# Dividing the softmax in the rows of `wo`: values and sums moved by DMA, reciprocal and product there, in place of two rounds of transposes

## The chip, the cores and the metric

The kernel runs on one core of a Trainium2 chip. The core has a matrix engine (TensorE, PE in the profile), three engines for elementwise work (VectorE or DVE, ScalarE or ACT, GpSimd or POOL), an engine that here only issues transfers (SyncE or SP) and 16 DMA engines. The metric is the time of one execution on the device in microseconds; lower is better. Everything is computed in float32.

## The reference

The input `x` has 8 sequences of 512 tokens with 256 features. Four residual blocks follow each other: attention with 16 heads of 16 features, a feed-forward block, a linear attention with a decay mask over groups of 512 tokens, and the same feed-forward block again. Only the first block bears on the change:

```python
q = x @ Wq + bq
kv = (x @ Wkv_down + bkv_down) @ Wkv_up + bkv_up
# split into k and v, 16 heads of 16 features; rotary embedding on q and k
att = jnp.einsum('bhqd,bhkd->bhqk', q, k) / jnp.sqrt(HEAD_DIM)
att = att + (log_sparse + jnp.log(decay + 1e-09))
att = jax.nn.softmax(att, axis=-1)          # the division of this softmax is what is changed
out = jnp.einsum('bhqk,bhkd->bhqd', att, v)
out = out + 0.2 * sigmoid(q . mean(k)) * mean(v)
return out.reshape(B, T, 256) @ Wo + bo
```

The division of the softmax is done after the product with `v`: a column of ones beside the values makes the same matmul give the sum of the unnormalised probabilities, and values are then divided by sums.

## The kernel before, in words

**Work items.** A batch (sequence) `b` has four groups `g` of four heads; item `i = 4 b + g` is one group, 32 items in all. A group has four blocks `t` of 128 tokens and two pairs of heads, so an item has 8 steps and the kernel has 256. In a step PE computes one pair's scores twice: `s` with queries in the rows, of which DVE takes the row maximum (`reduce_item`, tile `mr`), and, ten steps later for the same block and pair, `t` with keys in the rows, of which ACT takes the exponential into tile `p` (`soft_item`); DVE, or POOL in one step of three, then multiplies `p` by the table `dec_a`, two instructions of 128x512. Every second step `pv_item` adds a block's four heads into `pv`, one PSUM bank of 128 rows: 32 rows for each head, of which the first 16 are values and row 16 is the sum. `vaug` (tile `va`) is the stationary side of that matmul; in before a head has 17 columns in it, 16 values and a one. There is one `pv` bank.

**After an item.** `post_units(i)` makes the work that follows an item's last `pv` matmul. `evacuate` copies `pv` into `num` on ACT. `divide` turns `num` with four PE transposes (`flip`, line 201) into a PSUM tile with tokens in the rows, where the 16 sums of a token lie beside its values; a DVE reciprocal of 128x16 and a DVE product of 128x256 write `atok`. After every second item `turn` turns a half of `atok` back with four more transposes, and ACT copies the result into `aT`, features in the rows, as the product with `wo` wants it. `wo_unit` (two for each batch) then multiplies `aT` with `wo_sb`, adds the memory term (tiles `ga`, `me`), and DVE adds the residual.

**Order.** The order of instructions on each engine is fixed when the program is built: every instruction is pinned in program order. A planner at the end of the kernel decides it. It keeps a clock for each engine, and interleaves the 256 steps with chains of `Unit`s: the front of the next batches, the rest of earlier ones (feed-forward, linear attention), and `posts`, the units from `post_units`, which come first. A `Unit` names its estimated PE time, then the engines and nanoseconds that follow (`then`); units without PE time are issued as soon as the planner's PE clock comes within 300 ns of their start. `step_start` holds a step back until the planner's clocks say its PSUM banks and its `p` tiles are ready.

A unit may also have `needs`, names that another unit `gives`. A name is given at the moment at which the giving unit is issued, not at its estimated end:

```python
if any(x not in given for x in u.needs) or any(a.done is None for a in u.after):
    return None
...
t = max([a.done for a in u.after] + [clock["PE"] if u.pe else 0])
```

`wo_unit` stands in such a relation: `wos[0].needs = (("aT", b),)`, and the last unit of item `4 b + 3` gives `("aT", b)`.

**Transfers.** `move` (line 91) issues a DMA from SP's queue, in program order. It carries the loads, the way of rotated queries and keys through DRAM (`dq`, `dk`) and back into `qT` and `kT`, the loads of the next `x`, and the results. In PSUM, `s` and `t` share two tiles of two banks (`ps_sc`), one bank is `pv`, three are `misc`.

Of the kernel before, what the change touches and what calls it, by code (L numbers as in the profile page):

```python
# [9 lines left out]
F32 = mybir.dt.float32  # L10
AF = mybir.ActivationFunctionType
ALU = mybir.AluOpType
# [3 lines left out]
P = 128  # L16
B, T, D = 8, 512, 256
NH, HD = 16, 16
HH = 8
NG = 4  # L20
NT = T // P
NC = D // P
# [13 lines left out]
def tile_kernel(  # L36
# [37 lines left out]
    dve, act, gps = Engine(nc.vector), Engine(nc.scalar), Engine(nc.gpsimd)  # L74
# [4 lines left out]
    at = ctx.enter_context(tc.tile_pool(name="at", bufs=2))  # L79
    rs = ctx.enter_context(tc.tile_pool(name="rs", bufs=2))  # L80
# [9 lines left out]
    def move(to, src):  # L90
        tc.keep_in_program_order(nc.sync.dma_start(to, src))
# [11 lines left out]
    def keep(shape, name):  # L103
        return const.tile(shape, F32, tag=name, name=name)
# [24 lines left out]
    bv, b2 = row[:, 0, :], row[:, 1, :]  # L129
# [2 lines left out]
    qT = [keep([P, NG, T], f"qT{i}") for i in range(2)]  # L132
    kT = [keep([P, NG, T], f"kT{i}") for i in range(2)]

    vaug = [keep([P, NT, NH * 17 + 15], f"va{i}") for i in range(2)]

    mrow = [keep([P, NG, NT], f"mr{i}") for i in range(2)]

# [58 lines left out]
    def mm(o, l, r, start=True, stop=True):  # L197
        tc.keep_in_program_order(nc.tensor.matmul(o, lhsT=l, rhs=r, start=start, stop=stop))  # L198

    def flip(o, i):  # L200
        tc.keep_in_program_order(nc.tensor.transpose(o, i, ident))  # L201

    def misc(name):
        return ps_m.tile([P, 512], F32, tag="m", name=name)
# [39 lines left out]
    bb = const.tile([P, 5], F32, tag="bb", name="bb")  # L244
    wr = {}

    def plain(j):
        ps = misc(f"wr{j}")
        for o in range(NC):
            for c in range(NC):  # L250
                flip(ps[:, o * D + c * P : o * D + (c + 1) * P], wqk_in[:, c, j, o * P : (o + 1) * P])
        wr[j] = rs.tile([P, NC, D], F32, tag="xr", bufs=3, name=f"wr{j}")
        act.copy(wr[j].rearrange("p o d -> p (o d)"), ps)

    def product():
# [81 lines left out]
    def front1(b):  # L337
        def latent():
            ps = misc(f"lat_{b}")
            for c in range(NC):  # L340
                mm(ps[:LAT, :], wd_sb[:, c, :], xT_a[b]["xT"][:, c, :], c == 0, c == NC - 1)
            lt = fr.tile([LAT, T], F32, tag="lat", name=f"lat_{b}")
            lsum[b] = fr.tile([LAT, 1], F32, tag="lsum", name=f"lsum_{b}")
            act.activation(lt, ps[:LAT, :], AF.Identity, bias=vec[:LAT, V_BD : V_BD + 1], accum_out=lsum[b])
            lat_a[b] = lt

        def values(h):
            ps = misc(f"v_{b}_{h}")
            for i in range(2):
                t = 2 * h + i  # L350
                mm(ps[:, i * D : (i + 1) * D], lat_a[b][:, t * P : (t + 1) * P], wv_sb)
            for i in range(2):
                dve.tensor_tensor(
                    vaug[b % 2][:, 2 * h + i, : NH * 17].rearrange("p (h d) -> p h d", d=17)[:, :, :HD],
                    ps[:, i * D : (i + 1) * D].rearrange("p (h d) -> p h d", d=HD),
                    bv.rearrange("p (h d) -> p h d", d=HD),
                    ALU.add,
                )


        def mean_v():
            ps = misc(f"mv_{b}")
            for c in range(NC):
                mm(ps[:, c : c + 1], wv_sb[:, c * P : (c + 1) * P], lsum[b])
            m = fr.tile([P, NC], F32, tag="mv_a", name=f"mv_a_{b}")
            dve.scalar_tensor_tensor(m, ps[:, :NC], 0.1 / T, bvc, ALU.mult, ALU.add)
            for c in range(NC):
                gps.tensor_scalar(vmean[:, c, : NH + 1], vmask[:, c, :], m[:, c : c + 1], None, ALU.mult)

        def through_wo():  # L370
            ps = misc(f"me_{b}")
            for c in range(NC):
                mm(ps[:, :D], vmean[:, c, :], wo_sb[:, c, :], c == 0, c == NC - 1)
            dve.tensor_add(mem[b % 2][: NH + 1, :], ps[: NH + 1, :D], bo_row[: NH + 1, :])

        s, (h0, h1) = ln_units(lambda: xs[b], f"a{b}", fr)
        free = PER * (b - 1) + LAG + PVLAG + 2
        u = {"lat": Unit(latent, 1720, (("ACT", 700),), after=[h0[2], h1[2]])}
        for h in range(2):
            u["v", h] = Unit(  # L380
                lambda h=h: values(h), 900, (("DVE", 850),), after=[u["lat"]], step=free
            )
        u["mv"] = Unit(mean_v, 250, (("DVE", 150), ("POOL", 400)), after=[u["lat"]])
        u["me"] = Unit(through_wo, 900, (("DVE", 400),), after=[u["mv"]], needs=(("wo", b - 2),))
        xT_a[b] = s
        return h0 + h1, u
# [92 lines left out]
    probs, pv = {}, {}  # L479
# [38 lines left out]
    def pv_item(n):  # L518
        i, r = divmod(n, 8)
        t = r // 2  # L520
        if t == 0:
            pv[i] = ps_pv.tile([P, T], F32, tag="pv", name=f"pv_{i}")
        g, va = i % NG, vaug[(i // NG) % 2]
        for h in range(4):
            mm(
                pv[i][h * 32 : h * 32 + 32, :], va[:, t, (NG * g + h) * 17 : (NG * g + h) * 17 + 32], probs[(i, t, h // 2)][:, h % 2, :],
                t == 0, t == NT - 1,
            )
        probs.pop((i, t, 0)), probs.pop((i, t, 1))


    a_tok, aT = {}, {}

    def post_units(i):
        b, g = divmod(i, NG)
        s = {}

        def evacuate():
            num = at.tile([P, T], F32, tag="num", name=f"num_{i}")
            act.copy(num, pv[i])  # L540
            s["num"] = num

        def divide():
            if g == 0:
                a_tok[b] = at.tile([P, NT, D], F32, tag="atok", bufs=1, name=f"atok_{b}")
                aT[b] = at.tile([P, NC, T], F32, tag="aT", name=f"aT_{b}")
            ps = misc(f"num_{i}")
            for t in range(NT):
                flip(ps[:, t * P : (t + 1) * P], s["num"][:, t * P : (t + 1) * P])
            pn = ps.rearrange("p (t h d) -> p t h d", h=4, d=32)  # L550
            rd = at.tile([P, NT, 4], F32, tag="rd", name=f"rd_{i}")
            dve.reciprocal(rd, pn[:, :, :, HD])
            dve.tensor_tensor(
                a_tok[b][:, :, g * 64 : (g + 1) * 64].rearrange("p t (h d) -> p t h d", d=HD),
                pn[:, :, :, :HD], rd.unsqueeze(3).to_broadcast([P, NT, 4, HD]), ALU.mult,
            )

        def turn():
            c = g // 2
            ps = misc(f"aT_{i}")  # L560
            for t in range(NT):
                flip(ps[:, t * P : (t + 1) * P], a_tok[b][:, t, c * P : (c + 1) * P])
            act.copy(aT[b][:, c, :], ps)

        u = [Unit(evacuate, then=(("ACT", 600),))]
        u.append(Unit(divide, 520, (("DVE", 700),), after=u[-1:]))
        if g % 2:
            u.append(Unit(turn, 520, (("ACT", 600),), after=u[-1:], gives=("aT", b) if g == NG - 1 else None))
        return u


    def rest(b):
# [152 lines left out]
    for u in order0[:8]:  # L725
        u.fn()
    late_loads()
    plain(0), plain(1)
    for u in order0[8:12]:
        u.fn()  # L730
# [4 lines left out]
    clock = {"PE": 0, "DVE": 0, "ACT": 0, "POOL": 0}  # L735
# [9 lines left out]
    def start_of(u):  # L745
        if any(x not in given for x in u.needs) or any(a.done is None for a in u.after):
            return None
        if u.takes and held:
            return None
        t = max([a.done for a in u.after] + [clock["PE"] if u.pe else 0])  # L750
        return max(t, banks[0]) if u.bank else t

    def fetch(b):
        xs[b] = load_x(b)
        given.add(("x", b))

    def issue(u):
        t = start_of(u)
        u.fn()
        if u.pe:  # L760
            clock["PE"] = t = t + u.pe
        t += 100
        for e, ns in u.then:
            clock[e] = t = max(clock[e], t) + ns + 60
        u.done = t
        if u.bank:
            banks.popleft()
            banks.append(t)
        if u.takes:
            held.append(u)  # L770
        if u.frees:
            held.pop()
        if u.gives:
            given.add(u.gives)
            if u.gives[0] == "wo" and u.gives[1] + 3 < B:
                fetch(u.gives[1] + 3)
# [100 lines left out]
    t, credit, share = 0, 0, 0  # L877
    while t < LAST or any(chains) or posts:
# [11 lines left out]
        for rank, c in enumerate([posts] + chains):  # L890
            if not c or not c[0].pe or c[0].step > t:
                continue
            s = start_of(c[0])
# [16 lines left out]
        if take and best is None:  # L910

            c = min((c for c in [posts] + chains if c and start_of(c[0]) is not None), key=lambda c: start_of(c[0]))
# [121 lines left out]
```

## Time and profile before

| | |
|---|---|
| median of 3 runs | 1354.7 us (1354.05 to 1356.53) |
| the profiled execution's own time | 1355.33 us |
| its span in the profile | 1353.5 us |
| busy PE, DVE, ACT, POOL | 94%, 60%, 33%, 30% of the span |
| mean granted TensorE clock | 0.977 |
| SP's queue | 21446 packets, 30.83 MB |

The profile is of one execution; its span is 1.8 us shorter than the time of that execution, and that time is 0.6 us above the median. A group of instructions is told by engine, operation and `output<-input`, with the shape, the count, the busy time of the group, the mean duration in ns, and the idle time of the engine just before the group's instructions with what ended it. A float32 matmul appears as two records; a transpose as one. All elementwise instructions show line 69 and all transfers of SP line 91, since helpers record them, so groups are told apart by tiles.

### The profile page before, as it was taken

The numbers are of one execution on the slowest core, as the hardware profiler recorded it, in microseconds if no ns is written. First come the engines' busy times: TensorE is split into PE (matmuls) and PEld (weight loads), VectorE is DVE, ScalarE is ACT, GpSimd is POOL, SyncE is SP. The second block draws the span as 40 slices with busy tenths as digits, with TensorE's granted clock in tenths as the row PEclk, the third lists the DMA queues.
The fourth block names the chain that finished last, engine by engine and source line by source line (L and its number), as shares of the span: only waits on it lengthen the run. The fifth ranks groups of instructions, "written<-read, shape, count | busy, mean of one in ns | idle before, by whom it ended". The sixth has DMA issues, their size and how long they took to land. (4 is left out here: it accounts for less than half of the span.)

```text
span 1353.5 us, 15551 instructions
## 1 busy us (share of the span) xinstructions
PE 1278.4 (94%) x6116; PEld 632.2 (47%) x6116; DVE 805.8 (60%) x1323; ACT 450.8 (33%) x646; POOL 408.3 (30%) x461
## 2 busy tenths in 40 slices
PE   7889998999899998999999999999999999999989
PEld 3323233535354553545544454535444554455665
DVE  4577976678656686546765667646755484433120
ACT  2034434342434324333343323342343233331201
POOL 4165443233422323223331414213321232222010
PEclk9689989999999999999999999999999999999999
DMA  4440040003000210004000300003000000000000
GB/s 122 134 79 1 1 79 1 1 16 64 1 1 1 63 33 1 0 5 91 1 1 1 68 28 1 1 1 79 1 1 0 17 1 1 1 16 1 0 16 16
DMA packets 22159, 32.09 MB, mean 24 GB/s; under 512 B 2987, under 2 KB 12652, under 8 KB 21806
## 3 DMA queue, kind: packets, MB, share of 16 engines
q1 hardware_dynamic: 21446, 30.83, 10.2%
q8 instruction: 48, 0.79, 0.3%
q10 hardware_dynamic: 640, 0.26, 0.1%
q14 instruction: 25, 0.20, 0.0%
HBM read 18.24 MB, written 12.58 MB: 23 GB/s over the span
## 5 line engine op out<-in xcount | busy, mean ns | idle before, releaser
L69 DVE TENSOR_REDUCE mr<-s 128x2 f32<-128x1024 f32 x256 | 312.4, 1221 | 274.9 <-PE t L198 264.5
L69 ACT ACTIVATE p<-t 128x1024 f32<-128x1024 f32 (+1 forms) x290 | 264.0, 924 | 554.4 <-PE t L198 496.1
L69 POOL TENSOR_TENSOR p<-p,dec_a 128x512 f32<-128x512 f32 x182 | 233.1, 1302 | 490.0 <-ACT p L69 435.6
L198 PE MATMUL s<-kT,qT 32*128 32x512 f32 x1024 | 297.6, 664 | 40.3 <-DVE mr L69 36.5
L198 PE MATMUL t<-qT,kT 32*128 32x512 f32 x1024 | 297.0, 647 | 4.8 <-DVE mr L69 2.5
L69 DVE TENSOR_TENSOR p<-p,dec_a 128x512 f32<-128x512 f32 x330 | 230.1, 738 | 21.5 <-ACT p L69 21.3
L198 PE MATMUL x<-w_sb,h_x 128*128 128x256 f32 x1024 | 233.1, 383 | 0.0
L198 PEld LDWEIGHTS x<-w_sb,h_x 128*128 128x128 f32 x1024 | 190.7, 190 | 52.5 <-issue 27.6
L198 PEld LDWEIGHTS s<-kT,qT 32*128 32x128 f32 x1024 | 81.1, 189 | 208.1 <-DVE mr L69 85.2
L198 PE MATMUL pv<-p,va 128*32 128x512 f32 x1024 | 152.2, 614 | 3.7 <-DVE p L69 3.1
L69 ACT ACTIVATE h_x<-hx,vec 128x512 f32<-128x512 f32 x128 | 88.0, 688 | 156.3 <-PE hx L198 156.3
L198 PE MATMUL hx<-xT_g,w_sb 128*128 128x512 f32 x256 | 122.1, 622 | 0.7 <-ACT xT_g L69 0.7
L198 PE MATMUL hx<-xT_f,w_sb 128*128 128x512 f32 x256 | 119.0, 604 | 0.0
L69 DVE TENSOR_TENSOR x<-x,x 128x256 f32<-128x256 f32 x64 | 27.1, 424 | 153.9 <-PE x L198 153.8
L198 PEld LDWEIGHTS t<-qT,kT 32*128 32x128 f32 x1024 | 80.4, 184 | 22.0 <-issue 9.1
L198 PEld LDWEIGHTS hx<-xT_g,w_sb 128*128 128x128 f32 x256 | 48.0, 196 | 67.7 <-issue 59.8
L198 PEld LDWEIGHTS hx<-xT_f,w_sb 128*128 128x128 f32 x256 | 46.2, 192 | 57.5 <-issue 54.3
L198 PEld LDWEIGHTS pv<-p,va 128*32 128x32 f32 x1024 | 23.6, 108 | 78.2 <-issue 35.4
L69 POOL TENSOR_TENSOR x<-x,row 128x256 f32<-128x256 f32 x64 | 47.7, 765 | 38.4 <-DVE xn_g L69 20.4
L69 POOL TENSOR_TENSOR rc<-rc,rs 128x512 f32<-128x512 f32 x32 | 42.6, 1354 | 10.9 <-DVE rs L69 10.9
L198 PE MATMUL bs<-xT_r,ret 128*128 128x512 f32 (+3 forms) x128 | 38.3, 442 | 0.4 <-DVE mv_a L69 0.4
L198 PE MATMUL bo<-ret 128*128 128x256 f32 x160 | 36.7, 382 | 0.0
(130 smaller groups left out, 1034.5 us busy)
## 6 DMA issues: line engine op xcount, KB each, us to landing
dk<-rc SPq DMA_DIRECT2D x16, 256.0 KB
kT<-dk SPq DMA_DIRECT2D x32, 128.0 KB
dq<-rc SPq DMA_DIRECT2D x16, 256.0 KB
qT<-dq SPq DMA_DIRECT2D x32, 128.0 KB
out_dram<-x SPq DMA_DIRECT2D x32, 128.0 KB
x<-in_x_dram SPq DMA_DIRECT2D x7, 512.0 KB
w_sb<-in_w_dram SPq DMA_DIRECT2D x2, 1024.0 KB
x<-in_x_dram SPq DMA_DIRECT2D x2, 256.0 KB
```

What stands on the lines that cost most here:

```text
L69: ins = f(*a, **k)
L198: tc.keep_in_program_order(nc.tensor.matmul(o, lhsT=l, rhs=r, start=start, stop=stop))
```

## The change

Values and ones alternate in `vaug` now, 32 columns for each head (value, one, value, one, ...), so that `pv` has a value in each even row and the same head's sum in each odd row. `evacuate` still copies `pv` into `num`; two DMAs on SP's queue then move the 64 odd rows into a half of a new tile `den` and the 64 even rows into the matching half of `aT`, 128 KB each. After every second item, `divide` takes the reciprocal of the whole `den` tile, 128x512, and multiplies the chunk of `aT` by it, both on DVE. The transposes, `atok`, `rd`, and the ACT copy into `aT` are gone. The planner gets a new kind of entry, `(None, 2600)`, for the transfers' time, and an estimate of 1350 ns for the two DVE instructions. Two tiles of the setup (`wr`) move into a buffer that is used later, to make room.

```diff
-    vaug = [keep([P, NT, NH * 17 + 15], f"va{i}") for i in range(2)]
+    vaug = [keep([P, NT, 2 * D], f"va{i}") for i in range(2)]
...
             for i in range(2):
                 dve.tensor_tensor(
-                    vaug[b % 2][:, 2 * h + i, : NH * 17].rearrange("p (h d) -> p h d", d=17)[:, :, :HD],
-                    ps[:, i * D : (i + 1) * D].rearrange("p (h d) -> p h d", d=HD),
-                    bv.rearrange("p (h d) -> p h d", d=HD),
-                    ALU.add,
+                    vaug[b % 2][:, 2 * h + i, 0 : 2 * D : 2], ps[:, i * D : (i + 1) * D], bv, ALU.add,
                 )
...
         for h in range(4):
+            at_col = (NG * g + h) * 32
             mm(
-                pv[i][h * 32 : h * 32 + 32, :], va[:, t, (NG * g + h) * 17 : (NG * g + h) * 17 + 32], probs[(i, t, h // 2)][:, h % 2, :],
+                pv[i][h * 32 : h * 32 + 32, :], va[:, t, at_col : at_col + 32], probs[(i, t, h // 2)][:, h % 2, :],
                 t == 0, t == NT - 1,
             )
...
     def post_units(i):
         b, g = divmod(i, NG)
-        s = {}
+        c = g // 2
 
         def evacuate():
             num = at.tile([P, T], F32, tag="num", name=f"num_{i}")
             act.copy(num, pv[i])
-            s["num"] = num
+            if g == 0:
+                aT[b] = at.tile([P, NC, T], F32, tag="aT", name=f"aT_{b}")
+            if g % 2 == 0:
+                den[0] = at.tile([P, T], F32, tag="den", name=f"den_{b}_{c}")
+            rows_of = slice((g % 2) * 64, (g % 2) * 64 + 64)
+            move(den[0][rows_of], num[1:P:2])
+            move(aT[b][rows_of, c, :], num[0:P:2])
 
         def divide():
-            if g == 0:
-                a_tok[b] = at.tile([P, NT, D], F32, tag="atok", bufs=1, name=f"atok_{b}")
-                aT[b] = at.tile([P, NC, T], F32, tag="aT", name=f"aT_{b}")
-            ps = misc(f"num_{i}")
-            for t in range(NT):
-                flip(ps[:, t * P : (t + 1) * P], s["num"][:, t * P : (t + 1) * P])
-            pn = ps.rearrange("p (t h d) -> p t h d", h=4, d=32)
-            rd = at.tile([P, NT, 4], F32, tag="rd", name=f"rd_{i}")
-            dve.reciprocal(rd, pn[:, :, :, HD])
-            dve.tensor_tensor(
-                a_tok[b][:, :, g * 64 : (g + 1) * 64].rearrange("p t (h d) -> p t h d", d=HD),
-                pn[:, :, :, :HD], rd.unsqueeze(3).to_broadcast([P, NT, 4, HD]), ALU.mult,
-            )
-
-        def turn():
-            c = g // 2
-            ps = misc(f"aT_{i}")
-            for t in range(NT):
-                flip(ps[:, t * P : (t + 1) * P], a_tok[b][:, t, c * P : (c + 1) * P])
-            act.copy(aT[b][:, c, :], ps)
-
-        u = [Unit(evacuate, then=(("ACT", 600),))]
-        u.append(Unit(divide, 520, (("DVE", 700),), after=u[-1:]))
+            dve.reciprocal(den[0], den[0])
+            dve.tensor_mul(aT[b][:, c, :], aT[b][:, c, :], den[0])
+
+        u = [Unit(evacuate, then=(("ACT", 600), (None, 2600)))]
         if g % 2:
-            u.append(Unit(turn, 520, (("ACT", 600),), after=u[-1:], gives=("aT", b) if g == NG - 1 else None))
+            u.append(Unit(divide, then=(("DVE", 1350),), after=u[-1:], gives=("aT", b) if g == NG - 1 else None))
         return u
...
         for e, ns in u.then:
-            clock[e] = t = max(clock[e], t) + ns + 60
+            if e is None:
+                t += ns
+            else:
+                clock[e] = t = max(clock[e], t) + ns + 60
```

## The prediction, made before the changed kernel was run

> **What bounds the kernel now.** I read the busy times first, then the busy time by stretches, then the groups by form, the waits, and last the timeline of the engines around one `num` copy.
>
> ```profile
> PE 1278.4 (94%) x6116; PEld 632.2 (47%) x6116; DVE 805.8 (60%) x1323; ACT 450.8 (33%) x646; POOL 408.3 (30%) x461
> 100.00:200.00 100.00, 93.65 (x500) 34.05 (x492) 81.12 (x109) 42.85 (x78) 47.47 (x43) 0.95 0.16 31
> 500.00:600.00 100.00, 93.27 (x461) 40.73 (x460) 61.93 (x103) 39.80 (x54) 28.41 (x33) 0.98 0.00 1
> ```
>
> The columns of the last two are stretch, length, then busy PE, weight loads, DVE, ACT, POOL. PE's queue is the bound: it is busy 94%, the gaps on it sum to about 72 us, some 18 of them in the first 100 us. PE time removed is time won, and any wait of PE is time lost, since other work stands behind it in a fixed order. DVE is next, dense only early (81 of 100 us), later near 60.
>
> ```profile
> L201 PE MATMUL num<-ident,num 128*128 128x128 f32 x128 | 20.5, 284 | 0.0
> L201 PE MATMUL aT<-ident,atok 128*128 128x128 f32 x64 | 10.4, 286 | 0.5 <-DVE atok L69 0.5
> L69 ACT COPY num<-pv 128x512 f32<-128x512 f32 x32 | 18.6, 582 | 1.2 <-PE pv L198 1.2
> L69 ACT COPY aT<-aT 128x512 f32<-128x512 f32 x16 | 9.3, 579 | 0.8 <-PE aT L201 0.8
> L69 DVE RECIPROCAL rd<-num 128x16 f32<-128x16 f32 x32 | 7.9, 248 | 7.6 <-PE num L201 7.5
> L69 DVE TENSOR_TENSOR atok<-num,rd 128x256 f32<-128x256 f32 x32 | 13.6, 424 | 1.1
> L69 DVE TENSOR_TENSOR p<-p,dec_a 128x512 f32<-128x512 f32 x330 | 230.1, 738 | 21.5 <-ACT p L69 21.3
> L198 PE MATMUL wo<-wo_sb,aT 128*128 128x256 f32 x128 | 33.6, 384 | 0.4 <-ACT aT L69 0.4
> L69 DVE COPY bb<-bb x1: 165/165/165, 36.3 to 36.3; 128x5 f32<-128x5 f32 x1
> ```
>
> Here the reader sees the whole old path, and how little it waits: `wo` waited 0.4 us in all for `aT`, the transposes 0.5. The last row (minimum, median, maximum ns) is a tiny DVE copy out of PSUM, to set beside the reciprocal.
>
> The timeline around one `num` copy, DVE and ACT rows beside PE's and, from another place, SP's:
>
> ```profile
> 480.11 1.07 PE L198 MATMUL pv<-p,va 128*32 128x512 f32 x8
> 481.11 0.70 PE L198 MATMUL s<-kT,qT 32*128 32x512 f32 x2
> 482.18 3.27 PE L198 MATMUL bs<-xT_r,ret 128*128 128x512 f32 x8
> 485.29 0.60 PE L201 MATMUL num<-ident,num 128*128 128x128 f32 x4
> 485.82 0.70 PE L198 MATMUL s<-kT,qT 32*128 32x512 f32 x2
> ...
> 482.34 1.02 ACT L69 ACTIVATE p<-t 128x1024 f32<-128x1024 f32 x1 [4.64 <-PE t L198]
> 483.26 0.58 ACT L69 COPY num<-pv 128x512 f32<-128x512 f32 x1
> ...
> 468.50 2.20 SPq L91 DMA_DIRECT2D dq<-rc  x2
> 473.07 1.71 SPq L91 DMA_DIRECT2D qT<-dq  x4
> ```
>
> `pv` ends at 481.1, yet `num` is copied only from 483.26: the copy stands behind the exponential of the step that follows, and is done 2.7 us after `pv`. Four transposes hold PE from 485.29 to 485.82. On SP, the transfer back waits for both `dq` transfers (256 KB each, the second issued at 470.2) until 473.07, 2.9 us.
>
> **What the Trainium skill says.** "TensorE: Matmul & The Clock Gate" (Architectural detail: the array is 16× 32×32): TensorE can pull weight loads ahead of matmuls, DVE and ACT are strict first-in first-out; its section Step-by-step adds that matmuls stay in program order. The trace agrees: PE sat idle 36.5 us before `s` for DVE alone. "VectorE: DVE Perf Modes" (First, the fixed hardware budget): the reciprocal is an iterative divide with a repeat count of 8. The trace shows only 16 elements: 248 ns against 165 for the 5-element copy, dearer by an element, but less than 8 cycles. "DMA: Bandwidth & Descriptors" (Anatomy of one DMA) fits a transfer, there issued by GpSimd, as 2.0 us plus bytes over 436e3; 128 KB is then 2.3 us. The 2.9 us above, for 256 KB, agree roughly.
>
> **The change part by part.** It also re-plans the order, so I take the built program's order of instructions and price it with the durations above.
>
> *PE loses 48 groups of four transposes.* From the start of each to the start of the next group, the PE timeline gives 17.1 us for the 32 `num` groups and 8.0 us for the 16 `aT` groups, 0.52 each. With the 0.9 us of waits: **-26.0 us**. Matmuls with `va` keep their shapes.
>
> *ACT loses* 16 copies, 9.3 us; it is 33% busy and nothing waits for it at length, so nothing. *SP gains* 64 DMAs of 0.42 us issue (four `qT` issues took 1.71), 27 us on a queue that mostly waits; the transfers ahead of each pair in its queue (outputs, `x`) have their data by then, and `dk`, `dq` behind it are issued steps before use. I cost that at nothing; without this cover it would be 0.8 us at 32 places. Larger `va` memsets on POOL in the setup (1056 ns each, nearly twice the elements): up to 1 us, taken as nothing, other setup waits on loads. The `vaug` addition keeps its 256 elements; the `wr` tiles only move.
>
> *DVE* loses 32 x (248 + 424) = 21.5 us and gains 16 products and 16 reciprocals of 128x512. The product is a 128x512 `p` row, 0.74. The reciprocal is the open price. From below: all that the 16 elements cost above a copy is fixed, 0.08, beside 0.69 for a 512-element PSUM copy (`ct`): 0.77 us. From above: the skill's 8 cycles of 0.96 GHz, 4.3 + 0.16 = 4.4 us, an estimate. Middle: (248 - 150) / 16 = 6 ns an element, 3.1 + 0.16; I take **r = 3.2 us**, as the small one shows a slope and no large fixed part.
>
> *What waits.* `wo` needs `aT`, and the planner grants it when `divide` is issued, not when it is done. In the old order that cost one copy. In the new order `divide` has no PE time, so `wo` follows within a few matmuls, and PE stands until DVE has done what lies ahead, the reciprocal, the product. Example, batch 3, times from the end of the last `pv`: s,t 1.1; eight matmuls `x` (0.44 each) 4.6; s,t 5.7; four transposes 6.2; then `wo`. Data: exponential 2.2, `num` 2.8, two transfers 5.0 (2.2). DVE: ahead of the reciprocal stand the maximum of that second `s` (to 6.5) and the product `p`, whose exponential ends at 6.9 (to 8.2). Reciprocal to 11.4, product and semaphores (0.85) to 12.25: PE waits 6.05.
>
> | batch | PE is at `wo` | DVE at the reciprocal | aT ready | PE waits |
> |---|---|---|---|---|
> | 0 | 7.4 | 8.8 | 12.85 | 5.4 |
> | 1 | 6.95 | 6.95 | 11.0 | 4.05 |
> | 2 | 6.2 | 6.3 | 10.3 | 4.1 |
> | 3, 4 | 6.2 | 8.2 | 12.25 | 6.05 each |
> | 5 | 11.9 | 6.55 | 10.6 | 0 |
> | 6 | 10.7 | 8.3 | 12.4 | 2.05 |
> | 7 | 4.2 | 2.5 | 6.55 | 2.35 |
>
> (Batch 6 waits ahead of `wo`, for a bank of `bv` whose copy stands behind the product, at 12.75. Batch 7 has no step behind its `pv`.) Sum **+30.0 us**, which is 7 r + 7.6.
>
> The eight divisions after a batch's second item gate no `wo`; they delay the next maximum. In six of them 3 to 6 us of other matmuls come before that bank is wanted again: nothing. In batch 0 DVE is the bound, +3; in batch 6 two score steps stand together, +1.9. **+4.9 us**.
>
> Sum: -26.0 + 30.0 + 4.9 = +8.9 us on a profiled execution of 1355.33, which stood 0.6 above the median: **1364 us** as a median.
>
> **The rivals.** *A quick reciprocal* (ends on the other side): r is 0.77, DVE pipelines the divide. Then batches 0 to 4 wait 5 r + 9.6 = 13.4, 6 and 7 nothing, batch 0's other division 0.8: -26.0 + 14.2 = -11.8, 1343 us. For it: only 16 elements are seen, and the 83 ns may be fixed. Against: the skill's page. It decides where 8.5 r + 7.6 = 26, at r = 2.2. *The full 8 cycles*, r = 4.4: 8.5 x 1.2 = 10 more, 1374. *Late transfers*: landing counts only past DVE's own backlog, 3.2 us of cover in batches 3 and 4, 1.3 in batch 2, 2 in batch 1, none in 7. At 5 us instead of 2.2 that is some 6 us, 1370; SP's outputs ahead of a pair could do it. *The change not in effect*: the built order has 64 more DMAs and 16 wide reciprocals, and no `num` transposes, so no. *A re-planned order* moves other waits by a few us, either way.
>
> **How the numbers follow.** Forecast 0.47, 8 cycles 0.14, late transfers 0.06, all slower; quick reciprocal 0.25; between, near the break-even, 0.08. A measurement here can tell about 0.2%, 2.7 us. So slower 0.67, same 0.08, faster 0.25. The range reaches from the quick case to the dear one with a few us of re-planning: 1342 to 1378. The forecast's own is 1357 to 1371.
>
> **What would show it.** In the profile after: the group `aT`,`den` RECIPROCAL 128x512 with a mean near 3200 ns (rival 770); the idle time of PE before `wo<-wo_sb,aT` near 28 us, ended by DVE `aT`, against 0.4; no `num` transposes; the DMAs into `den` and `aT` landed about 2.2 us after issue, and DVE not idle before the reciprocal except in batch 7. A `wo` wait under 10 us, or a reciprocal under 2.2 us, would make the forecast wrong.

## The result, and the profile after

| | before | after |
|---|---|---|
| median of 4 runs each | 1355.15 us | 1385.31 us (1383.34 to 1386.25) |
| ratio, 95% interval | | 1.022 [1.0202, 1.0238] |
| profiled execution, own time and span | 1355.33, 1353.5 us | 1386.03, 1384.2 us |
| PE busy | 1278.4 us | 1270.8 us |
| gaps on PE, summed from the trace | 71.6 us | 109.9 us |
| mean granted TensorE clock | 0.977 | 0.962 |

The changed kernel is slower by 30.2 us; the prediction said 9 us, in a range that ended at 1378. The first lines are from the page of after, the busy times and two of its costliest groups.

```profile
PE 1270.8 (92%) x5924; PEld 617.6 (45%) x5924; DVE 849.2 (61%) x1291; ACT 442.9 (32%) x630; POOL 412.9 (30%) x461
...
L198 PE MATMUL wo<-wo_sb,aT 128*128 128x256 f32 x128 | 40.7, 438 | 24.6 <-DVE aT L69 24.6
...
L69 DVE RECIPROCAL den<-den 128x512 f32<-128x512 f32 x16 | 53.5, 3346 | 4.4 <-DMA den<-num 4.3
```

Three things are to be seen. The wide reciprocal takes 3346 ns (3.2 us were taken). PE stood idle 24.6 us before `wo`, released by DVE (0.4 before). And the same 128 matmuls of `wo` take 438 ns each, where they took 384 in before: no forecast step changed that duration.

The product of values and inverted sums, in the groups by form of after:

```profile
L69 DVE TENSOR_TENSOR aT<-aT,den 128x512 f32<-128x512 f32 x16 | 12.6, 785 | 0.5
```

The stretches that were shown of before, in after (stretch, length, busy PE, weight loads, DVE, ACT, POOL, then the granted clock):

```profile
100.00:200.00 100.00, 87.05 (x416) 29.10 (x416) 76.19 (x93) 37.85 (x71) 42.77 (x36) 0.87 0.13 33
500.00:600.00 100.00, 97.64 (x474) 45.44 (x478) 65.52 (x107) 38.49 (x51) 28.50 (x34) 1.00 0.06 14
```

From 100 to 200 us PE is busy for 6.6 us less than in before, and its clock is 0.87 there, against 0.95. The stretch from 500 has no end of a batch in it, no wait at `wo`, and is better than before. Fixed stretches no longer hold the same work, so they show where to look, not what is lost.

Now batch 3, the worked example of the prediction. The timeline of PE, and of DVE for the same time:

```profile
619.37 1.06 PE L198 MATMUL pv<-p,va 128*32 128x512 f32 x8
...
626.16 0.66 PE L201 MATMUL tr_r<-ident,xn_r 128*128 128x128 f32 x4
626.65 0.60 PE L198 MATMUL wo<-wo_sb,aT 128*128 128x256 f32 x2
632.76 1.22 PE L198 MATMUL wo<-wo_sb,aT 128*128 128x256 f32 x2 [5.52 <-DVE aT L69]
633.78 1.06 PE L198 MATMUL wo<-me,ga 128*128 128x256 f32 x2
634.63 1.92 PE L198 MATMUL wo<-wo_sb,aT 128*128 128x256 f32 x4
...
627.43 1.29 DVE L69 TENSOR_TENSOR p<-p,dec_a 128x512 f32<-128x512 f32 x2
628.64 3.35 DVE L69 RECIPROCAL den<-den 128x512 f32<-128x512 f32 x1
632.02 0.69 DVE L69 TENSOR_TENSOR aT<-aT,den 128x512 f32<-128x512 f32 x1
```

`pv` ends at 620.4. DVE comes to the reciprocal 8.2 us later and is done with the product 12.3 us later, as the prediction had it (8.2 and 12.25). PE waits 5.5 us instead of 6.05, because the first two `wo` matmuls read the half of `aT` that was divided two items earlier. And then: two `wo` matmuls took 0.60 us at 626.65 and 1.22 us at 632.76. The same kernel by stretches around this wait:

```profile
625.00:630.00 5.00, 2.25 (x15) 1.00 (x14) 4.16 (x5) 1.50 (x2) 0.00 (x0) 1.00 0.13 45
630.00:632.00 2.00, 0.00 (x0) 0.00 (x0) 1.99 (x1) 0.00 (x0) 0.00 (x0) 0.81 0.00 0
632.00:635.00 3.00, 2.24 (x5) 1.85 (x6) 0.69 (x1) 0.00 (x0) 0.00 (x0) 0.50 0.00 0
635.00:640.00 5.00, 5.00 (x23) 2.13 (x22) 0.85 (x2) 0.10 (x1) 0.00 (x0) 0.69 0.00 0
```

The granted clock falls to half while PE stands and stays there until about 638.1, when PE has been at work again for 5.3 us: work that is done at half speed. The wait cost 5.5 us, and then about 2.7 us more.

**The ledger.** PE's gaps grew by 38.3 us: 24.2 before `wo`, 2.0 before `bv`, 10.3 before `s` for row maxima (36.5 to 46.8), 1.8 elsewhere. PE's busy time fell by only 7.6 us, though the transposes that went took 25.1. So the matmuls that stayed became 17.5 us longer. Differences of the groups' busy times say where: `wo` from `aT` +7.1, `wo` from `me` +2.8, `s` +3.5 (with `t` beside it), `x` +2.8, `pv` +1.4, which makes 17.6 (smaller changes of other groups, up and down, are left out). The clock says why: 1 - 0.977 of 1353.5 us is 31.1 us of full clock missing in before, 1 - 0.962 of 1384.2 is 52.6 in after, 21.5 more, part of it while PE was idle. From the trace's clock records, the stretches at half clock that lie whole inside the span sum to 61.3 us in before and 105.5 in after. Only those parts in which PE is busy make its matmuls longer: laid over PE's busy time, they are 56.2 us in before and 90.5 in after, and half of the difference is 17.1 of the 17.5 us. 38.3 - 7.6 = 30.7 us, the whole difference of the spans.

### The profile page after: what moved, and what is told of

Same layout as the page of the kernel before. It is cut to its first block, busy times and chain, and to the rows that moved or that the text cites. A ratio compares the mean times of both kernels' runs of the same rounds, so it can differ in the third digit from the quotient of the medians.

```text
span 1384.2 us, 15259 instructions
## 1 busy us (share of the span) xinstructions
PE 1270.8 (92%) x5924; PEld 617.6 (45%) x5924; DVE 849.2 (61%) x1291; ACT 442.9 (32%) x630; POOL 412.9 (30%) x461
## 5 line engine op out<-in xcount | busy, mean ns | idle before, releaser
L198 PE MATMUL s<-kT,qT 32*128 32x512 f32 x1024 | 301.1, 671 | 50.7 <-DVE mr L69 46.8
L198 PE MATMUL t<-qT,kT 32*128 32x512 f32 x1024 | 300.4, 654 | 4.6 <-DVE mr L69 2.4
L69 DVE TENSOR_TENSOR p<-p,dec_a 128x512 f32<-128x512 f32 x330 | 231.8, 744 | 22.6 <-ACT p L69 22.6
L198 PE MATMUL x<-w_sb,h_x 128*128 128x256 f32 x1024 | 235.9, 386 | 0.0
L198 PEld LDWEIGHTS t<-qT,kT 32*128 32x128 f32 x1024 | 81.4, 187 | 21.5 <-issue 6.4
L198 PE MATMUL wo<-wo_sb,aT 128*128 128x256 f32 x128 | 40.7, 438 | 24.6 <-DVE aT L69 24.6
L69 DVE RECIPROCAL den<-den 128x512 f32<-128x512 f32 x16 | 53.5, 3346 | 4.4 <-DMA den<-num 4.3
```

What stands on the lines that cost most here:

```text
L69: ins = f(*a, **k)
```

## The experiments

Each was timed against the kernel before on the same chip, whose median was 1354.7 to 1356.8 us there. Gaps and half-clock stretches come from the trace of the one profiled execution, and executions of one kernel differ: the timed executions of before have mean clocks of 0.971 to 0.979, which is 57 to 79 us at half clock, those of after 0.959 to 0.963, which is 102 to 114. So a difference of 20 us or less in the last column can be chance.

| kernel | us | ratio, interval | gaps on PE | before `wo` on `aT` | before `s`, `t` on `mr` | at half clock |
|---|---|---|---|---|---|---|
| before | 1355.15 | | 71.6 | 0.4 | 39.0 | 61.3 |
| after | 1385.31 | 1.022 [1.0202, 1.0238] | 109.9 | 24.6 | 49.2 | 105.5 |
| wo planned at the division's end | 1373.44 | 1.0135 [1.0108, 1.0162] | 93.8 | 2.2 | 52.3 | 95.3 |
| true estimate alone | 1384.67 | 1.0203 [1.0173, 1.0233] | 104.8 | 18.2 | 49.0 | 98.7 |
| both | 1373.44 | 1.0132 [1.0107, 1.0157] | 92.8 | 0 | 53.2 | 102.1 |
| a copy for the reciprocal | 1362.75 | 1.0052 [1.0032, 1.0072] | 88.4 | 8.4 | 46.4 | 88.5 |
| waits filled | 1374.71 | 1.0146 [1.0128, 1.0165] | 85.1 | 1.1 | 48.8 | 81.7 |
| copy, and wo at its end | 1342.45 | 0.9902 [0.9878, 0.9926] | 77.1 | 0 | 41.7 | 78.3 |
| before, with 16 unread reciprocals | 1368.31 | 1.0095 [1.0078, 1.0113] | 74.5 | 0.4 | 42.2 | 81.7 |
| before, in another order | 1356.19 | 1.0015 [1.0002, 1.0027] | 72.5 | 0.5 | 42.1 | 71.5 |
| reciprocal in four parts | 1362.3 | 1.0048 [1.003, 1.0067] | 92.9 | 0 | 53.6 | 95.3 |
| narrow reciprocal by way of DRAM | 1398.45 | 1.0314 [1.0291, 1.0336] | 103.5 | 0 | 59.5 | 139.7 |
| the same, planned longer | 1382.71 | 1.0191 [1.017, 1.0212] | 105.0 | 2.2 | 55.2 | 102.1 |

### A copy in place of the reciprocal

```diff
-            dve.reciprocal(den[0], den[0])
+            dve.tensor_copy(den[0], den[0])
```

> After the change with a plain DVE copy of the same 128x512 tile in place of the reciprocal, in the same order; the output is not normalised, so only the time is meant. The copy is put at 0.45 us against 3.35. Theory A: waits at wo fall from 24.6 us by about 2.9 us in seven batches to 6 to 10, the two delayed maxima lose 4.5, and the clock losses behind these waits (10 to 15 us) go: 1348 to 1358. Theory B: only waits go, 1362 to 1367. Theory C' (the transfers and the new order are the loss, whatever the reciprocal): 1375 or more.

1362.75 us, in the range of theory B and not of A. The kernel leaves the division out, so only its time is of use. It is 22.6 below after, and the wait at `wo` falls from 24.6 to 8.4 us. This is one step of DVE shortened from 3.35 to 0.55 us in the same order of instructions, so three quarters of the loss belongs to its length. What was saved is gaps, which are 21.5 us shorter; PE's busy time fell by only 1.6 us. Theory A expected the clock to recover with the shorter waits, but waits at `wo` of 2.2 to 2.6 us were still followed by 3.4 us at half clock (from 181.5, 621.9 and 778.9 us on). PE still idles 44.0 us before `s` for `mr` (36.5 in before, 46.8 in after). One of these gaps, 2.69 us up to 1137.42 in after, is there with the copy too, and in after the last division before it ended near 1107. Most of the growth before `s` came with the rest of the change, above all its new order, and not with the long reciprocal.

### The waits filled with matmuls that nobody reads

```diff
+            if h == 0:
+                for _ in range((9, 7, 8, 12, 12, 0, 0, 5)[b]):
+                    mm(ps[:, :D], wo_sb[:, 0, :P], wo_sb[:, 1, :])
```

> After the change with matmuls of 128x256 that nobody reads, put ahead of the first wo of batches 0, 1, 2, 3, 4 and 7 (9, 7, 8, 12, 12 and 5 of them, 0.44 us each, a little less than the measured waits of 4.4, 3.3, 3.6, 5.5, 5.5 and 2.2 us). PE then works where it waited; nothing comes earlier. Theory A: the half-clock stretches at 177, 324, 631 and 792 us, 27 us long, do not appear, which gives 9 to 12 us: 1373 to 1377, and the mean granted clock goes from 0.962 to about 0.972. Theory B (the wait alone is the loss, the clock only goes with it): 1384 to 1387, or more where the matmuls overshoot.

1374.71 us, as theory A had it. The kernel does 53 matmuls more than after, waits for the same reciprocals, and ends 10.6 us earlier. From its groups by form:

```profile
L198 PE MATMUL wo<-wo_sb,aT 128*128 128x256 f32 x128 | 34.5, 385 | 1.2 <-DVE aT L69 1.1
```

A `wo` matmul takes 385 ns again (438 in after, 384 in before), and half-clock stretches shrink by 23.8 us, which is 11.9 us at full speed. Of the four stretches that were to go, those at 324, 631 and 792 us are gone; of the one at 177, 10.2 us long, 3.4 us stay, behind a wait for a row maximum. That PE's idleness itself made the later matmuls slow is shown by this: no data came earlier, only PE wasn't idle.

### The permission and the estimate

The three kernels change the planner. The first lets `wo` start only at the planned end of the division:

```diff
+    ended = {}
...
-        t = max([a.done for a in u.after] + [clock["PE"] if u.pe else 0])
+        t = max([a.done for a in u.after] + [clock["PE"] if u.pe else 0] + [ended.get(x, 0) for x in u.needs])
...
+            if u.gives[0] == "aT":
+                ended[u.gives] = u.done
```

> After the change (1385.3 us) with one edit in the planner: the first wo unit of a batch may start only at the estimated end of its division (1350 ns for the two DVE instructions), no longer at its issue. Theory A (two losses: PE waits at wo, 24.6 us, and each long wait lets the granted clock fall to a half for some us, about 17 us of lost PE time): PE gets other work while DVE divides, the estimate is 2.7 us short, so waits at wo fall to 8 to 14 us and half of the lost clock returns: 1358 to 1366 us. Theory B (only the waits count, the rest of the loss comes from the re-planned order): 1370 to 1378. Theory C (the division's DVE time itself, not the place of wo, is the loss): 1383 to 1388.

The second changes the estimate alone:

```diff
-            u.append(Unit(divide, then=(("DVE", 1350),), after=u[-1:], gives=("aT", b) if g == NG - 1 else None))
+            u.append(Unit(divide, then=(("DVE", 4150),), after=u[-1:], gives=("aT", b) if g == NG - 1 else None))
```

> The changed kernel with the planner's estimate of a division set to what it takes (4150 ns on VectorE instead of 1350); the output projection is still allowed from the moment the division is issued. Theory A, the wait belongs to the permission and not to the estimate: the waits at wo stay near 24 us and the time at 1376 to 1390. Theory B, the estimate alone mends it, since the planner keeps other work on VectorE away: waits at wo under 12 us, 1362 to 1374, like the kernel with both edits (1373.4).

The third has both:

> As the run before it, and the division's estimate raised from 1350 to 4150 ns, what the two DVE instructions take (3.35 + 0.69 us and their start). Theory A: waits at wo under 4 us, lost clock near that of the kernel before (32 us of half-clock loss in its span): 1334 to 1346 us, faster than before (1355.2) by about the 25 us of removed transposes less what the maxima are delayed. Theory B: 1355 to 1365. Theory C: 1380 or more.

The true estimate alone does nothing to the time (1384.67), and 18.2 us of waits at `wo` stay in its profiled execution, the fastest of its four (1379.20): most of the wait belongs to the permission. The permission takes nearly all of the wait away and wins 11.9 us, less than theory A had and inside theory B's range. The estimate on top wins nothing more, and 1373.44 lies in none of the ranges that were expected of the kernel with both. Where the rest stays, the groups by form of the kernel with both say:

```profile
L198 PE MATMUL t<-qT,kT 32*128 32x512 f32 x1024 | 303.2, 659 | 12.8 <-DVE mr L69 10.5 <-DVE va L69 2.2
L198 PE MATMUL s<-kT,qT 32*128 32x512 f32 x1024 | 301.7, 673 | 50.4 <-DVE mr L69 42.7 <-DMA qT<-dq 4.3 <-ACT p L69 3.3
```

`t` waits 10.5 us for row maxima (2.5 in before, 2.4 in after), with single gaps of 3.58 and 3.52 us. In the 5 us after the eight divisions that gate `wo`, PE waits 13.6 us for maxima; in after it doesn't wait there for any. The block of 4 us on DVE no longer holds `wo`, it holds the maxima that stand behind it in DVE's order. Half-clock stretches stay at 102.1 us.

### The copy, with wo at its end

```diff
-            dve.reciprocal(den[0], den[0])
+            dve.tensor_copy(den[0], den[0])
...
-            u.append(Unit(divide, then=(("DVE", 1350),), after=u[-1:], gives=("aT", b) if g == NG - 1 else None))
+            u.append(Unit(divide, then=(("DVE", 1200),), after=u[-1:], gives=("aT", b) if g == NG - 1 else None))
```

(with the permission of the kernel above)

> The planner edit that lets wo start only at the division's estimated end, estimate 1200 ns, and a DVE copy in place of the reciprocal (output not normalised; only the time is meant). It has neither the wait at wo nor the long DVE instruction, but all 64 transfers and the new order. Theory A (DVE's 3.35 us blocks delay the maxima and so PE, and each delay also costs clock; that kept the run with the full estimate at 1373): nothing of this is left, the 25 us of transposes come through: 1333 to 1345 us. Theory B (transfers or the re-planned order cost as much as the transposes did): 1355 to 1363, as with the copy in the old plan (1362.8).

1342.45 us, as theory A had it, and 12.3 below before. This kernel, too, leaves the division out. So 64 more transfers, the interleaved `vaug`, the product and a new order leave the transposes' gain standing, when what DVE does between is short. Only 12 of the 26 us arrive: gaps are still 5.5 us longer than in before, and PE's busy time is 18.3 us lower, not 25.1.

```profile
PE 1260.1 (94%) x5924; PEld 610.8 (46%) x5924; DVE 811.2 (61%) x1291; ACT 443.4 (33%) x630; POOL 415.8 (31%) x461
```

Half-clock stretches with PE busy are 14.2 us longer, 7.1 at full speed, which would cover the missing 6.8 (its four mean clocks are 0.966 to 0.970, those of before beside them 0.972 to 0.979).

### The kernel before, with the reciprocals added

```diff
             act.copy(aT[b][:, c, :], ps)
+            dve.reciprocal(junk, junk)
```

> The kernel before, with one DVE reciprocal of 128x512 on a tile that nobody reads, put behind the second transposes of every second item: 16 of them, 3.35 us each, 54 us of DVE time, that the planner does not know of. No wo waits for them, no transfer is added, all transposes stay. Theory A (a DVE block delays the maxima and PE with them): 10 to 25 us slower, 1365 to 1380, with more idle PE before s and a lower mean clock than 0.977. Theory B (DVE, 60% busy, hides it): 1353 to 1358.

1368.31 us, 13.6 above before and in theory A's range. Nobody waits for these results; from its groups by form and its page:

```profile
L69 DVE RECIPROCAL junk<-junk 128x512 f32<-128x512 f32 x16 | 53.5, 3342 | 0.0
```

```profile
PE 1288.2 (94%) x6116; PEld 634.8 (46%) x6116; DVE 852.5 (62%) x1339; ACT 450.9 (33%) x646; POOL 409.1 (30%) x462
```

PE's gaps grew by only 2.9 us, its busy time with the same matmuls by 9.8 (1278.4 to 1288.2), and half-clock stretches by 20.4. The four executions of this kernel have mean clocks of 0.970 to 0.972, those of before beside them 0.972 to 0.979. The price of these blocks on DVE came mostly as slower matmuls, and no list of waits shows it.

### How much an order alone moves

```diff
-        u.append(Unit(divide, 520, (("DVE", 700),), after=u[-1:]))
+        u.append(Unit(divide, 520, (("DVE", 900),), after=u[-1:]))
...
-            u.append(Unit(turn, 520, (("ACT", 600),), after=u[-1:], gives=("aT", b) if g == NG - 1 else None))
+            u.append(Unit(turn, 520, (("ACT", 800),), after=u[-1:], gives=("aT", b) if g == NG - 1 else None))
```

> The kernel before with nothing changed but two of the planner's estimates (a transposing division 900 ns instead of 700 on VectorE, the second turn 800 instead of 600 on ScalarE), so that the same instructions stand in another order from the first division on. It shows how far an order alone moves the time. Theory A, orders of this planner are alike: 1350 to 1360. Theory B, a new order alone brings or takes 10 us and more: outside 1345 to 1365; then differences of that size between two kernels of different order can't be put down to one edit.

1356.19 us, 0.15% more by the ratio and in theory A's range. Another order of before moved the time by about 2 us (0.3 to 3.7 by the interval). It is one other order only, but the differences of 10 us and more above aren't of that size. It also shows how far a sum of half-clock time can be trusted: PE is busy at half clock for 10.4 us more than in before, and yet its busy time is the same (1278.4), so such a sum is good to about 5 us.

### The reciprocal in four parts

```diff
-            dve.reciprocal(den[0], den[0])
+        def part(j):
+            def invert():
+                cols = slice(j * P, (j + 1) * P)
+                dve.reciprocal(den[b, c][:, cols], den[b, c][:, cols])
...
+            for j in range(NT):
+                u.append(Unit(part(j), then=(("DVE", 880), (None, 400)), after=u[-1:]))
```

(with the permission of the kernels above; parts and product stand in a list of the planner's own)

> The changed kernel with the output projection planned at the division's end, and the reciprocal of each half cut into four of 128x128 (about 0.85 us each by the 3.35 us of the whole), each a step of its own that the planner places about 1.3 us apart in a list of its own, then the product. The work on VectorE is that of the kernel with both edits of the planner (1373.4); only the block of 4 us is cut up. Theory A, it is the length of one block ahead of the row maxima that stalls TensorE and drops its clock: 1343 to 1358, TensorE idle before s and t on mr near the 41 us of the kernel with the copy, half-clock stretches under 85 us in all. Theory B, it is VectorE's added time whatever its pieces: 1366 to 1380, idle before s and t over 48 us.

1362.3 us, 11.1 below the uncut kernel with both edits, and it fits neither theory. From its groups by form:

```profile
L69 DVE RECIPROCAL den<-den 128x128 f32<-128x128 f32 x64 | 59.5, 938 | 4.4 <-DMA den<-num 4.4
L198 PE MATMUL s<-kT,qT 32*128 32x512 f32 x1024 | 301.6, 672 | 55.8 <-DVE mr L69 50.6 <-DMA qT<-dq 4.3 <-ACT p L69 0.6
```

DVE works 6 us more on reciprocals (59.5 against 53.5) and yet 11 us are won. The parts were also planned from a list of their own, which gives a new order, and no run tells the two edits apart. The idle time before `s` and `t` is the same (53.6 and 53.2 us); it lies in more and shorter gaps, and the two of 3.5 us before `t` are gone. PE's busy time is 9.4 us lower (1264.2 against 1273.6); half-clock stretches shrink by 6.8 us, 3.4 at full speed, which is within chance. What makes up the 9.4 isn't settled. It is the best of the kernels here that do the whole division in the rows of `wo`, and is still 0.48% slower than before.

### A narrow reciprocal by way of DRAM

The eight sums of a half go to DRAM, come back as 128x32, are inverted there and spread over the rows by one more transfer:

```diff
+            move(s["sum"], d_sum[0].rearrange("h (c f) -> (h c) f", f=8 * T // P))
...
+            dve.reciprocal(s["sum"], s["sum"])
...
+            move(s["inv"].rearrange("h (c f) -> (h c) f", f=8 * T // P), s["sum"])
...
+            move(s["den"], s["inv"].unsqueeze(1).to_broadcast([8, HD, T]))
```

(with the permission of the kernels above)

> A version meant to be faster: the values go by DMA into aT as after the change, but of the sums only one row for each head is moved, through DRAM into a tile of 128x32 for two items; the reciprocal is taken there (32 elements in a row, put at 0.35 us), goes back through DRAM, and is spread over the 16 rows of each head by the last transfer; then the product. The planner knows each leg (2300 to 2600 ns) and lets wo start at the product's end. Theory A: DVE gives up 54 us of reciprocals, wo has other work ahead of it: 1332 to 1346 us. Theory B (four legs in SP's queue, each waiting for the one before, hold up the queries' and keys' way): 1358 or more, with idle PE before s ended by DMA.

1398.45 us, the slowest of all, with a reciprocal of 0.34 us. Theory A is out. The time fits theory B, but its sign isn't there: what ends PE's long waits is DVE, not a transfer (the 4.3 us for `qT<-neg` are two waits of about 2 us). The groups by form:

```profile
L198 PE MATMUL t<-qT,kT 32*128 32x512 f32 x1024 | 304.8, 663 | 23.9 <-DVE mr L69 17.3 <-DMA qT<-neg 4.3 <-DVE va L69 2.2
L69 DVE TENSOR_TENSOR aT<-aT,den 128x512 f32<-128x512 f32 x16 | 11.3, 709 | 21.1 <-DMA den<-di 15.5 <-issue 5.6
```

Here DVE itself stands, 15.5 us in four waits of up to 9.1, at a product whose sums haven't come back, and the row maxima stand behind it: `t` waits 17.3 us for them. The second version plans the transfers longer, in a list of their own:

```diff
-        u = [Unit(evacuate, then=(("ACT", 600), (None, 2300)))]
+        u = [Unit(evacuate, then=(("ACT", 600), (None, 4000)))]
...
-            u.append(Unit(gather, then=((None, 2300),), after=u[-1:]))
-            u.append(Unit(invert, then=(("DVE", 350), (None, 2300)), after=u[-1:]))
-            u.append(Unit(spread, then=((None, 2600),), after=u[-1:]))
+            u.append(Unit(gather, then=((None, 4000),), after=u[-1:]))
+            u.append(Unit(invert, then=(("DVE", 350), (None, 4000)), after=u[-1:]))
+            u.append(Unit(spread, then=((None, 6000),), after=u[-1:]))
...
-                posts.extend(us)
+                posts.extend(us[:1])
+                divs.extend(us[1:])
```

> The narrow reciprocal by way of DRAM again (128x32 for the eight sums of a half, then spread by a transfer), with the transfers planned at 4, 4, 4 and 6 us instead of 2.3, 2.3, 2.3 and 2.6, and these steps in a list of their own, so that no other step of the planner is held behind them. Theory A, the first narrow version was slow because VectorE stood in order at products whose sums had not landed (15.5 us, four times up to 9.1 us), and row maxima behind them: 1336 to 1356, VectorE's wait at the product on den's transfer under 3 us, TensorE's idle before t on mr under 3 us. Theory B, it is the added traffic on SyncE's queue (three more transfers each half, each waiting in order ahead of the loads of q and k): 1375 to 1400, with that wait gone all the same.

1382.71 us. DVE's wait at the product fell to 2.6 us and `t`'s for maxima to 3.6, and 15.7 us came back. They didn't come back as gaps, which sum to 105.0 us against 103.5, but as busy time of PE, 17.1 us lower, with half-clock stretches 37.6 us shorter. The list of their own changed the order too, so how much of it the wait alone was worth isn't shown. The rest, 26 us above before, falls in the range of theory B. That SyncE's queue is its cause wasn't shown: PE's gaps are many small ones (51.6 us before `s`), and none is ended by a transfer of `q` or `k` at length. It stays open.

## Why the prediction was wrong in size

**Right: the reciprocal.** 3346 ns against r = 3.2 us; the quick rival (770 ns) and the full 8 cycles (4.4 us) are both out. **Right: the mechanism of the wait.** The permission at issue puts `wo` ahead of its data; moving the permission took the wait from 24.6 to 2.2 us. By batch:

| batch | 0 | 1 | 2 | 3 | 4 | 5 | 6 (`bv`) | 7 |
|---|---|---|---|---|---|---|---|---|
| predicted | 5.4 | 4.05 | 4.1 | 6.05 | 6.05 | 0 | 2.05 | 2.35 |
| measured | 4.4 | 3.3 | 3.6 | 5.5 | 5.5 | 0 | 2.0 | 2.2 |

26.5 us instead of 30.0, the first five shorter by 0.5 to 1 us. In batch 3 this is the two `wo` matmuls on the other half of `aT`, which the example left out.

**Nearly right: the transfers.** In batch 7, the one case in which DVE was idle at the reciprocal, the timeline of SP and DVE in after has

```profile
1239.82 0.48 SPq L91 DMA_DIRECT2D den<-num  x1
...
1242.58 3.35 DVE L69 RECIPROCAL den<-den 128x512 f32<-128x512 f32 x1 [4.26 <-DMA den<-num]
```

which is 2.3 us from the end of the issue to the start of the reciprocal, and 2.8 from its start (2.2 were expected). The late-transfer rival is out.

**Right in sum: the eight other divisions.** The step allowed 4.9 us before the next maxima; in the 5 us after these divisions PE waits 5.4 us for maxima in after. Batch 0's 3.0 us was as predicted. That the sum came out is luck in part: the 1.9 us predicted in batch 6 isn't there, and 1.9 us stands in batch 7, where none was predicted. **Too small: the rest of the waits before `s`.** In all they grew by 10.3 us, and what lies behind none of these divisions comes with the new order more than with the reciprocal, as the kernel with the copy showed. All waits together came to 38.3 us of added gaps, where the prediction's steps make 34.0 (30.0 + 4.9 - 0.9).

**The step that failed: a wait was priced at its own length.** "PE time removed is time won, and any wait of PE is time lost" left out what a wait does to the matmuls after it. The sum had -26.0 + 30.0 + 4.9; in its place stand -25.1 for the transposes, +38.3 for the gaps, and a term that was absent, +17.5 for matmuls at half clock, together 30.7. The missing term is four fifths of the miss; the filled waits gave 10.6 us of it back without an earlier datum, so that much is the price of the waits at `wo`. The other 7 us weren't traced to single waits. The material for it was at hand: the page "TensorE: Matmul & The Clock Gate" of the Trainium skill (What's actually happening), which the prediction used for something else, says that the clock falls to 4/8 after at least one idle window of about 3.4 us and needs about as long a busy one to return, and the profile of before showed a clock below 1. Five predicted waits of 4 to 6 us should have been priced with it. In after the clock is at half when four of these five waits end. The rival of a re-planned order, a few us either way, came on top: the growth before `s` is mostly of that kind.

## What to carry to other kernels

On a matmul-bound queue, price a stall of 2 us and more twice: its length, and the matmuls after it at half clock, which here lasted 3.4 us or a multiple; compare the mean duration of unchanged matmul groups (here 384 and 438 ns) before believing a list of waits. A planner that grants data when its producer is issued is safe only while the producer is short. When a long elementwise instruction is taken out of one waiter's way, ask who stands behind it next on the same engine: here it was the row maxima. The kernel with the division in four parts lost less than the one with 4 us at once on DVE, though its order differed too.

## What the runs showed of the hardware

**A gap of 2 us can drop the clock, and one of 3.6 us need not.** The Trainium skill's page "TensorE: Matmul & The Clock Gate" (Why this matters for your kernels) warns of gaps over some 3 us. Four stretches of after, around a gap of 3.63 us that ends at 475.99 and one of 2.05 us that ends at 1266.6:

```profile
473.00:476.00 3.00, 0.01 (x1) 0.01 (x1) 2.97 (x3) 0.00 (x0) 0.00 (x0) 1.00 0.00 0
476.00:480.00 4.00, 4.00 (x26) 2.28 (x26) 1.51 (x5) 0.00 (x0) 3.01 (x4) 1.00 0.00 0
...
1267.00:1269.50 2.50, 1.22 (x8) 0.82 (x8) 2.12 (x5) 0.58 (x1) 2.50 (x5) 1.00 0.00 0
1269.50:1273.00 3.50, 3.50 (x6) 1.37 (x5) 1.02 (x5) 0.74 (x2) 2.89 (x5) 0.51 0.00 0
```

After 3.63 us of idleness the clock stayed at 1.00; after 2.05 us and a further 1.3 us in small pieces around it, the clock fell to half for 3.4 us, when PE was fully busy again. All half-clock stretches that lie inside the span last about 3.4 us or a multiple, and in each of the 13 traces here all of them begin on one grid of 3.413 us. That fits the window that runs freely on the same page (What's actually happening). Cut along this grid, the traces tell what share of idleness is enough. These are the pieces of all 13 that begin at full clock, the first 20 us left out, by how much of the piece PE is busy:

| PE busy in the piece | pieces | next piece at half clock |
|---|---|---|
| under 40% | 96 | 96 |
| 40 to 50% | 49 | 38 |
| 50 to 80% | 440 | 29 |
| 80% and more | 4176 | 1 |

The gap of 3.63 us fell on two pieces, busy for 45% and 49%, and passed. The one of 2.05 us fell on two pieces as well, busy for 54% and 49%, and after the second the clock dropped. So a gap's place on the grid counts, not its length alone; what decides between 40 and 50% isn't shown.

**The reciprocal grows by 6.25 ns an element of the free dimension**: 346 ns for 32 elements (the second narrow kernel, median) and 3346 for 512, so (3346 - 346) / 480; the 938 ns for 128 lie within 8 ns of that line. The prediction's 6 ns from the small PSUM one was close. The Trainium skill's page "VectorE: DVE Perf Modes" (First, the fixed hardware budget) has a repeat count of 8; at the 0.96 GHz that the prediction used, the slope is 6.0 cycles, so taking that count for 8 cycles an element was too dear.
